# Token layer of a four-layer conv network: the residual in two half tiles, each loaded for the next chunk

## The chip, the cores and the metric

The kernel runs on one core of one Trainium2 chip. The metric is the device time of one launch in microseconds (us). All data is 32-bit float. A core has a matmul engine (PE, with its weight loads PEld), a vector engine (DVE), a scalar engine for activations (ACT), a general engine (POOL) and an engine that here only issues DMAs (SP). Each engine takes its instructions in the order in which the built program lists them, and waits where one of them needs what another engine or a DMA has not yet made.

## The reference

Four layers work on an image of 4 x 48 x 256 x 256. Each normalizes its input over 16 groups of channels and adds its result to that input. The second, the token layer, is the one that changes:

```python
t = x.reshape(B, H * W, dim)                       # 48 consecutive numbers of x are one token
t = gelu(gelu(t @ W1 + b1))                        # 48 -> 16, exact gelu
x1, x2 = t[..., :8], t[..., 8:]
n = layernorm(x2)                                  # over 8 features, then seen as 8 images of 256 x 256
sp = depthwise 3x3 conv(n) + dw_b
ch = 1x1 conv(n) + pw_b
out = (x1 * (sp * ch)) @ W2 + b2                   # 8 -> 48
...
x = x + _L1_conv_ref(_gn(x), ...)                  # the residual: the layer's own input, once more
```

The first layer is a channel attention with 3x3 depthwise convolutions. Layers three and four run recurrences over the rows and the columns of the image.

## The kernel before, in words

The program runs in three stretches. The first computes the attention weights of layer one. The second applies layer one as a convolution in blocks of 16 rows and, from the second image on, runs the token layer of the images that are done beside it. The third is a long recurrence on PE (`ps` L1010) for layers three and four.

In the second stretch a token layer's unit is a chunk of 32 image rows. There are 8 chunks to an image and 32 in all. `tick(c, conv)` returns pieces that are emitted one after the other. Tick c works on three chunks at once. It transposes the tokens of chunk c+1 (`load`, `relay`, `transposed`). It computes the hidden features and the norm of chunk c (`hidden`, `centered`, `normed`). For chunk `old` = c-2 it computes the gate and the output (`shift`, `gate`, `add_b2`, `output`, `finish`). Between them it calls `conv` four times, and each call emits half of a block of layer one, until the blocks run out. So the first 20 ticks that have an output hold two blocks of layer one each, and the last 12 hold the token layer alone.

The order within one engine is not simply the order of emission: the framework reorders instructions by its own estimate of when they can start. All DMAs here go through SP's one queue.

The names that matter:

- `x1` is the layer's input in memory; `load(c)` reads a chunk of it as tokens into `tok` (L726, 1.5 MB in two DMAs, one buffer), `relay` copies it to `pairs` on POOL (L733), `transposed` turns it by PE (`ptok` L739) into `xt` (copies L743 on ACT, L745 on DVE).
- `hidden`: PE `ph` L686, ACT `h` L756, L765, L767. `centered`: PE `pm` L773, DVE `d` L775, POOL `sq` L777. `normed`: PE `pvar` L782, ACT `v` L784, DVE reciprocal L785, DVE `d` L787, ACT `n` L789, then the `near<-n` DMAs L799 to L808.
- `gate`: PE `psp` L818 and L819 (L819 reads `nears`, which POOL fills at L812), PE `pch` L821, ACT `sp` L824, DVE `sp` L825, POOL `g` L827.
- `load_x(c)` reads the chunk's residual into `xr` (L835, two DMAs of 768 KB, one buffer of 96 x 4096). Its partitions hold two image rows of a pair times 48 channels; the free axis holds 16 pairs of rows.
- `add_b2(c)` adds the output bias to the whole tile in place (ACT, L839).
- `output(c, ip)` is called for the even pairs (`ip` 0) and the odd pairs (`ip` 1). It makes four matmuls `pout` into four of the seven PSUM banks (L853) and eight DVE sums `y<-pout,xr` (L864). After `ip` 1 the chunk is written (L872) and `finish` takes its statistics (L883).
- Layer one: `x1n` and `x2n` are the normalized inputs (POOL memsets L527, L528; ACT L529; one buffer each), PE `py` L569 and L578, DVE `y` L592 and statistics L593, DMAs `t<-in_x` L510 to L523 and `x<-y` L598.

Of the kernel before, what the change touches and what calls it, by code (L numbers as in the profile page):

```python
# [9 lines left out]
F32 = mybir.dt.float32  # L10
# [6 lines left out]
B, C, H, W = 4, 48, 256, 256  # L17
G = 16
NP = 2
P = 96  # L20
HW = H * W
R = 16
NB = H // R
RT = 32
KC = 8
# [611 lines left out]
def gated_layer(ctx, tc, banks, p_small, x1, x2, w1, w2, dw, ends, pw, cols, b2, k, coef1, coef2):  # L637
# [6 lines left out]
    nc = tc.nc  # L644
# [3 lines left out]
    res = ctx.enter_context(tc.tile_pool(name="t_res", bufs=1))  # L648
# [4 lines left out]
    items = [(b, j) for b in range(B) for j in range(NJ)]  # L653
# [45 lines left out]
    def strips(b):  # L699

        got = []
        for c in range(2):
            spread = feat.tile([P, G], F32, tag="spread", name="spread")
            nc.vector.tensor_scalar_mul(spread, k["of_group", P], coef1[b][:, c : c + 1])
            ps = p_small.tile([128, G], F32, tag="small", name="pstrip")
            nc.tensor.matmul(ps, lhsT=k["ones", P], rhs=spread, start=True, stop=True)
            t = feat.tile([128, G], F32, tag=f"strip{c}", name=f"strip{c}")
            nc.vector.tensor_copy(t, ps)
            got.append(t)
        scale[b] = got[0]  # L710
        bias[b] = feat.tile([128, 2, G], F32, tag="bias", name="bias")
        for half in range(2):
            nc.vector.tensor_scalar(
                bias[b][:, half, :], got[1], csum[:, half : half + 1], col[:, half : half + 1], ALU.mult, ALU.add
            )

    toks, pairs, xts = {}, {}, {}
    h1s, h2s, ds, sqs, gs, xrs, ys, stats = {}, {}, {}, {}, {}, {}, {}, {}

    def load(c):  # L720
        b, j = items[c]
        t = toks[c] = tok.tile([128, R, 4 * C], F32, tag="tok", name="tok")
        flat = x1[b].rearrange("c n -> (c n)")[j * 2 * R * W * C : (j + 1) * 2 * R * W * C]
        src = flat.rearrange("(k r t n) -> k t r n", k=2, r=R, t=T)
        for kk in range(2):
            nc.sync.dma_start(t[kk * T : (kk + 1) * T], src[kk])  # L726

    def relay(c):

        m = pairs[c] = tok.tile([128, 4, R, C], F32, tag="pairs", name="pairs")  # L730
        t = toks.pop(c).rearrange("p r (q e) -> p q r e", q=4)
        for r in (0, R // 2):
            nc.gpsimd.tensor_copy(m[:, :, r : r + R // 2, :], t[:, :, r : r + R // 2, :])  # L733
# [15 lines left out]
    def hidden(c, half):  # L749
        b, j = items[c]  # L750
        ph = banks.tile([128, CH], F32, tag="bank", name="ph")
        project(ph, half, lambda t: xts[c, t])
        h = feat.tile([128, CH], F32, tag=f"hid{half}", name="h")
        for kk in range(2):
            g = 2 * j + kk
            nc.scalar.activation(  # L756
                by_token(h)[:, kk],
                by_token(ph)[:, kk],
                AF.Gelu,
                bias=bias[b][:, half, g : g + 1],  # L760
                scale=scale[b][:, g : g + 1],
            )
        if half == 0:
            h1 = h1s[c] = feat.tile([128, 2, W], F32, tag="h1", name="h1", bufs=4)
            nc.scalar.activation(h1.rearrange("p k (t q) -> p k q t", q=4), by_token(h), AF.Gelu)  # L765
        else:
            nc.scalar.activation(h, h, AF.Gelu)  # L767
            h2s[c] = h

    def centered(c):  # L770
        pm = banks.tile([128, CH], F32, tag="bank", name="pm")
        h2 = h2s.pop(c)
        nc.tensor.matmul(pm, lhsT=k["mean8", 128], rhs=h2, start=True, stop=True)  # L773
        d = ds[c] = feat.tile([128, CH], F32, tag="d", name="d")
        nc.vector.tensor_sub(d, h2, pm)  # L775
        sq = sqs[c] = feat.tile([128, CH], F32, tag="sq", name="sq", bufs=1)
        nc.gpsimd.tensor_mul(sq, d, d)  # L777
# [32 lines left out]
    def shift(c):  # L810
        for dx in range(3):
            nc.gpsimd.tensor_copy(shifted[c % 2][32 * dx : 32 * dx + 2 * F], near[c % NN][:, :, dx : dx + W])  # L812
# [13 lines left out]
        g = gs[c] = feat.tile([128, 2, W], F32, tag="g", name="g")  # L826
        nc.gpsimd.tensor_mul(flat(g), flat(h1s.pop(c)), sp)  # L827

    def load_x(c):
        b, j = items[c]  # L830
        t = xrs[c] = res.tile([P, 2, R // 2, W], F32, tag="xr", name="xr")
        src = x1[b].rearrange("c (h w) -> c h w", w=W)[:, 2 * j * R : 2 * (j + 1) * R, :]
        src = src.rearrange("c (k i r) w -> r c k i w", k=2, r=2)
        for r in range(2):
            nc.sync.dma_start(t[r * C : (r + 1) * C], src[r])  # L835

    def add_b2(c):
        t = xrs[c]
        nc.scalar.activation(t, t, AF.Identity, bias=b2_sb)  # L839

    def output(c, ip):
        b, j = items[c]
        if ip == 0:

            ys[c] = res.tile([P, NK, 2, R, KC], F32, tag="y1", name="y1")
            if j == 0:
                stats[b] = feat.tile([P, NJ * 8, 6], F32, tag="st", name="st1")
        y, t, g = ys[c], xrs[c], gs[c]
        ps = []
        for q in range(4):  # L850
            p = banks.tile([P, 2, W], F32, tag="bank", name="pout")
            here = slice(32 * q, 32 * q + 32)
            nc.tensor.matmul(  # L853
                p.rearrange("p k (q v) -> p k q v", q=2),
                lhsT=w2_sb[here, ip, :],
                rhs=g[here].rearrange("p k (v q) -> p k q v", q=2),
                start=True,
                stop=True,
            )
            ps.append(p)  # L860
        for q in range(4):
            i = 2 * q + ip
            for kk in range(2):
                nc.vector.tensor_add(  # L864
                    y[:, :, :, kk * R // 2 + i, :].rearrange("p a q w -> p q a w"),
                    ps[q][:, kk].rearrange("p (q a w) -> p q a w", q=2, a=NK),
                    t[:, kk, i, :].rearrange("p (a w q) -> p q a w", w=KC, q=2),
                )
        if ip == 0:
            return  # L870
        gs.pop(c)
        nc.sync.dma_start(  # L872
            x2[b // 2][:, b % 2, :, j * R : (j + 1) * R, :].rearrange("p a h w -> p a (h w)"),
            y.rearrange("p a q h w -> p (a q) (h w)"),
        )
# [3 lines left out]
    def finish(c):  # L879
        b, j = items[c]  # L880
        flat = ys.pop(c).rearrange("p a q h w -> p (a q h w)")
        for i in range(8):
            nc.vector.bn_stats(stats[b][:, j * 8 + i, :], flat[:, i * 512 : (i + 1) * 512])  # L883
        if j == NJ - 1:
            mv = feat.tile([P, 2], F32, tag="mv1", name="mv1")
            nc.vector.bn_aggr(mv, stats.pop(b).rearrange("p a b -> p (a b)"))
            after.extend(k.group_norm_pieces(feat, p_small, mv, "mean6", coef2[b]))

    def tick(c, conv):

        n, old = len(items), c - 2
        now, was, new = 0 <= c < n, 0 <= old < n, c + 1 < n

        def first():
            if c < 0:
                load(c + 1)
            if new:  # L900
                relay(c + 1)
            if was:
                load_x(old)
                shift(old)
            while after:
                after.pop(0)()

        def last():
            if c + 2 < n:
                load(c + 2)  # L910

        pieces = [first]
        if now:
            if items[c][1] == 0:
                pieces.append(lambda: strips(items[c][0]))
            pieces += [lambda: hidden(c, 1), lambda: hidden(c, 0)]
        if was:
            pieces.append(lambda: gate(old))
        pieces.append(conv)
        if now:  # L920
            pieces.append(lambda: centered(c))
        if new:
            pieces += [lambda i=i: transposed(c + 1, i) for i in range(2)]
        if was:
            pieces += [lambda: add_b2(old), lambda: output(old, 0)]
        pieces.append(conv)
        if new:
            pieces += [lambda i=i: transposed(c + 1, i) for i in range(2, 4)]
        if now:
            pieces.append(lambda: normed(c))  # L930
        if was:
            pieces.append(lambda: output(old, 1))
        pieces.append(conv)
        if new:
            pieces += [lambda i=i: transposed(c + 1, i) for i in range(4, NI)]
        if was:
            pieces.append(lambda: finish(old))
        pieces += [conv, last]
        if c == n + 1:
            pieces.append(lambda: [piece() for piece in after])  # L940
        return pieces
# [503 lines left out]
```

## Time and profile before

| what | value |
|---|---|
| median of 4 runs | 9557.14 us (9549.5 to 9560.55) |
| the profiled execution's own time | 9560.55 us |
| its span from first to last instruction | 9558.5 us |
| mean granted clock of PE | 0.957 |
| PE busy | 8768.3 us, 92% of the span |
| DVE, ACT, POOL busy | 4395.0, 3317.3, 1449.0 us |
| first `xr` load to last sum of the token layer | 2107 to 3564 us |
| chunk writes L872 in ticks with layer one | 20, from 2143.3 to 3180.1 us |
| chunk writes L872 in ticks without | 12, to 3564.4 us |

The rows of the profile give an engine, a line of the program, the tile written and the tiles read, a count, and what ended the idle time before. PE's busy time contains modelled ends and so overstates how full it is. The clock that PE was granted is given in parts of full speed.

### The profile page before, as it was taken

To read this page: it belongs to the slowest core of one execution; us is meant where nothing else is said; L and a number is where in the kernel's file an instruction comes from. 1 tells how busy PE (TensorE), PEld (TensorE's weight loads), DVE (VectorE), ACT (ScalarE), POOL (GpSimd) and SP (SyncE) were. 2 spreads that over 40 slices of the span, in tenths; PEclk is the share of its full clock that TensorE was granted. 3 is DMA by queue.
4 is the path that set the end of the run, shared out by engine and by line. 5 is a ranking of instruction groups with operands and counts; after the bars stand their busy time and mean duration, and the time that the engine had idled before them with its cause. 6 is when DMAs were issued, how large, how long until landed. Compare 5 with 4: busy or idle time off the path is not lost.

```text
span 9558.5 us, 160394 instructions
## 1 busy us (share of the span) xinstructions
PE 8768.3 (92%) x62920; PEld 7269.5 (76%) x62920; DVE 4395.0 (46%) x10806; ACT 3317.3 (35%) x7021; POOL 1449.0 (15%) x2850
## 2 busy tenths in 40 slices
PE   6999999989999759999999999999999999976980
PEld 5777777333333229999999999999999999966980
DVE  3331011335554554445556665556655555533550
ACT  0000010223333437546652246632256622243101
POOL 0000000001111110000003320023300033311460
PEclk9999999999999879999999999999999999987995
DMA  7653322668888768656647776557676567588669
GB/s 153 132 127 79 69 67 60 134 140 176 172 173 177 155 133 154 144 126 163 150 123 183 192 158 161 140 146 189 169 163 157 141 151 193 145 194 195 168 175 200
DMA packets 1033974, 1440.81 MB, mean 151 GB/s; under 512 B 63952, under 2 KB 955600, under 8 KB 965632
## 3 DMA queue, kind: packets, MB, share of 16 engines
q1 hardware_dynamic: 1033120, 1430.22, 65.7%
q8 instruction: 493, 8.08, 0.4%
q14 instruction: 265, 2.17, 0.1%
q0 software_dynamic: 96, 0.33, 0.0%
HBM read 837.19 MB, written 534.77 MB: 144 GB/s over the span
## 4 chain that ended last, share of the span: by engine, by line
PE 85%; DMA 7%; DVE 2%; SPq 2%; ACT 2%; issue 1%; POOL 0%; ACTq 0%; DVEq 0%; POOLq 0%
PE ps L1010 57%; PE py L569 5%; PE acc L283 5%; PE acc L284 5%; PE acc L285 3%; PE py L578 3%; DMA col<-U 2%; DMA oi<-x 2%; DMA tok<-x 2%; PE pt L265 1%; DMA xr<-x 1%; PE ptok L739 1%; PE ph L686 1%; PE pout L853 1%; ACT xr L839 1%
## 5 line engine op out<-in xcount | busy, mean ns | idle before, releaser
L1010 PE MATMUL ps<-carry,w 96*96 96x128 f32 x48960 | 5522.0, 275 | 191.0 <-DVE carry L1018 163.9
L1010 PEld LDWEIGHTS ps<-carry,w 96*96 96x96 f32 x48960 | 5432.4, 163 | 279.9 <-DVE carry L1018 187.7
L1018 DVE SCALAR_TENSOR_TENSOR carry<-ps,b,col 96x128 f32<-96x128 f32 x4080 | 1787.6, 440 | 1335.7 <-PE ps L1010 1141.7
L1221 POOL TENSOR_TENSOR stage<-stage,carry 96x128 f32<-96x128 f32 (+1 forms) x2044 | 1060.4, 520 | 4225.7 <-DVE carry L1018 4106.5
L1191 ACT COPY col<-carry 96x128 f32<-96x128 f32 x2040 | 845.3, 425 | 774.4 <-DVE carry L1018 763.6
L1131 ACT COPY up<-carry 96x128 f32<-96x128 f32 x1792 | 528.3, 298 | 1537.5 <-DVE carry L1014 1537.3
L1014 DVE TENSOR_TENSOR carry<-ps,dn 96x128 f32<-96x128 f32 x2280 | 656.2, 288 | 750.1 <-PE ps L1010 631.2
L1090 ACT ACTIVATE dn<-carry,b 96x128 f32<-96x128 f32 (+1 forms) x2044 | 791.9, 399 | 332.5 <-DVE carry L1014 282.6
L569 PE MATMUL py<-x1n,wy 128*96 128x512 f32 x1536 | 717.7, 617 | 33.8 <-ACT x1n L529 29.2
L1014 DVE TENSOR_TENSOR carry<-ps,up 96x128 f32<-96x128 f32 x1792 | 509.2, 287 | 503.9 <-ACT up L1131 376.8
L284 PE MATMUL acc<-xs,xt 128*96 128x288 f32 x2048 | 667.0, 408 | 0.0
L283 PE MATMUL acc<-xt 128*96 128x288 f32 x2048 | 666.3, 409 | 0.0
L569 PEld LDWEIGHTS py<-x1n,wy 128*96 128x96 f32 x1536 | 249.5, 169 | 470.6 <-issue 452.6
L268 DVE COPY xt<-pt 128x384 f32<-128x384 f32 x256 | 136.6, 554 | 851.1 <-PE pt L265 651.2
L285 PE MATMUL acc<-xt,xs 128*96 128x192 f32 x2048 | 501.8, 327 | 0.0
L250 ACT ACTIVATE xn<-raw,coef 96x2048 f32<-96x2048 f32 x64 | 133.6, 2094 | 986.0 <-PE pt L265 819.0
L285 PEld LDWEIGHTS acc<-xt,xs 128*96 128x96 f32 x2048 | 332.3, 165 | 154.5 <-issue 1.8
L284 PEld LDWEIGHTS acc<-xs,xt 128*96 128x96 f32 x2048 | 332.1, 165 | 151.2 <-issue 2.4
L592 DVE TENSOR_TENSOR y<-py,t 96x512 f32<-96x512 f32 x256 | 169.9, 678 | 439.4 <-PE py L578 439.4
L578 PE MATMUL py<-x2n,wy 64*96 64x512 f32 x1536 | 361.9, 601 | 6.7 <-ACT x2n L529 6.7
L283 PEld LDWEIGHTS acc<-xt 128*96 128x96 f32 x2048 | 330.5, 165 | 5.6 <-issue 1.5
L578 PEld LDWEIGHTS py<-x2n,wy 64*96 64x96 f32 x1536 | 117.7, 159 | 239.3 <-issue 238.4
(176 smaller groups left out, 4163.9 us busy)
## 6 DMA issues: line engine op xcount, KB each, us to landing
stage<-x SPq DMA_DIRECT2D x64, 1536.0 KB
x<-stage SPq DMA_DIRECT2D x64, 1536.0 KB
dn<-x SPq DMA_DIRECT2D x240, 384.0 KB
col<-U SPq DMA_DIRECT2D x60, 1536.0 KB
R<-col SPq DMA_DIRECT2D x60, 1536.0 KB
col<-R SPq DMA_DIRECT2D x60, 1536.0 KB
D<-dn SPq DMA_DIRECT2D x56, 1536.0 KB
up<-D SPq DMA_DIRECT2D x56, 1536.0 KB
```

What stands on the lines that cost most here:

```text
L283: nc.tensor.matmul(acc[0], lhsT=xt[:, h + 2, :], rhs=xt[:, here, :], start=first, stop=last)
L284: nc.tensor.matmul(acc[1], lhsT=xt[:, h + 2, :], rhs=xs[:, here, :], start=first, stop=last)
L285: nc.tensor.matmul(acc[2], lhsT=xs[:, h + 2, :], rhs=xt[:, past, :], start=first, stop=last)
L569: nc.tensor.matmul(ps, lhsT=held["w"][0][:, dx], rhs=x1n[:, 2 * c : 2 * c + 2, dx : dx + W], start=dx == 0, stop=False)
L578: nc.tensor.matmul(held["ps"][q + 2 * s], lhsT=held["w"][1][here, dx], rhs=x2n[here, 2 * q : 2 * q + 2, dx : dx + W], start=False, stop=dx ...
L1010: nc.tensor.matmul(ps, lhsT=w_sb[layer][:, way, j, :], rhs=old[:, i, j : j + W // 2], start=j == 0, stop=j == 2)
L1014: nc.vector.tensor_add(new[:, i].rearrange("p (k w) -> p k w", w=KC), ps.rearrange("p (k w) -> p k w", w=KC), inp[:, i])
L1018: nc.vector.scalar_tensor_tensor(new[:, i], ps, b_sb[layer][:, way : way + 1], inp[:, i], ALU.add, ALU.add)
L1090: nc.scalar.activation(inp[:, b], blocks(new[:, b]), AF.Identity, bias=bias[:, 0:1])
L1131: nc.scalar.copy(place[:, b], blocks(new[:, b]))
L1191: nc.scalar.copy(col[:, b], new[:, b])
L1221: nc.gpsimd.tensor_add(to[:, b], to[:, b], new[:, b])
```

## The change

The tile `xr` becomes two half tiles of 96 x 2048, one for the pairs of each parity (`xr0`, `xr1`), with one buffer each. `load_x(c, ip)` fills one of them by two DMAs of 384 KB. It is no longer called at the start of the tick that uses it. `output(c, ip)` calls it for chunk c+1 after it has emitted the eight sums that read the half tile. The first chunk's halves are loaded at the end of tick 1. `add_b2` works on each half by itself. The bytes, the matmuls and the sums are the same.

```diff
-    def load_x(c):
+    def load_x(c, ip):
+        if c >= len(items):
+            return
         b, j = items[c]
-        t = xrs[c] = res.tile([P, 2, R // 2, W], F32, tag="xr", name="xr")
+        t = xrs[c, ip] = res.tile([P, 8, W], F32, tag=f"xr{ip}", name="xr")
         src = x1[b].rearrange("c (h w) -> c h w", w=W)[:, 2 * j * R : 2 * (j + 1) * R, :]
-        src = src.rearrange("c (k i r) w -> r c k i w", k=2, r=2)
+        src = src.rearrange("c (q i r) w -> i r c q w", i=2, r=2)
         for r in range(2):
-            nc.sync.dma_start(t[r * C : (r + 1) * C], src[r])
-    def add_b2(c):
-        t = xrs[c]
+            nc.sync.dma_start(t[r * C : (r + 1) * C], src[ip, r])
+    def add_b2(c, ip):
+        t = xrs[c, ip]
         nc.scalar.activation(t, t, AF.Identity, bias=b2_sb)
...
-        y, t, g = ys[c], xrs[c], gs[c]
+        y, t, g = ys[c], xrs.pop((c, ip)), gs[c]
...
-                    t[:, kk, i, :].rearrange("p (a w q) -> p q a w", w=KC, q=2),
+                    t[:, 4 * kk + q, :].rearrange("p (a w q) -> p q a w", w=KC, q=2),
                 )
+        load_x(c + 1, ip)
         if ip == 0:
             return
...
             if was:
-                load_x(old)
                 shift(old)
...
         def last():
+            if old == -1:
+                for ip in range(2):
+                    load_x(0, ip)
             if c + 2 < n:
                 load(c + 2)
...
-            pieces += [lambda: add_b2(old), lambda: output(old, 0)]
+            pieces += [lambda: [add_b2(old, ip) for ip in range(2)], lambda: output(old, 0)]
```

In the changed program the line numbers of the touched steps are L838 (load), L842 (bias), L856 (`pout`), L867 (sums), L876 (chunk write) and L887 (statistics).

The framework's reordering gives the changed program these orders on the engines. They are read from the built programs.

- PE, ticks with layer one: before, `pm` L773 stood between the first quarter's L569 and L578; now it stands after L578.
- DVE, the same ticks: `d<-h,pm` L775 stood ahead of that quarter's two `y` L592 and two statistics L593; now it stands behind them. The eight sums of `ip` 0 stand behind the next `xt` copy L745, and three of `ip` 1 stand ahead of the reciprocal L785.
- ACT, the same ticks: the block's `x1n` L529 stood ahead of `sp` L824; now it stands behind it. The next block's `x1n` and `x2n` stand ahead of `v` L784. One half's bias stands between `v` and `n` L789, the other between the last `xt` copy and the first `h`; both belong to the next chunk.
- SP, the same ticks: `tok` x2, seven `t` loads, `xr0` x2, `x<-y` x2, one `t` load, `near` x4, `xr1` x2, the chunk write, six `t` loads, `x<-y` x2.
- Ticks without layer one: both biases stand ahead of `v` L784 (before: one, behind `n` L789). On DVE the sums of `ip` 0 stand ahead of the reciprocal in some ticks and behind it in others, those of `ip` 1 behind `d` L787. On PE L819 stands behind `pch`, `pm` and the first `ptok`. On SP `tok` stands behind the chunk write.

## The prediction

> **What bounds it now.** The chain that ended last says which engine to watch: PE has 85% of it, and the residual's load appears at 1%. I then asked the tile `xr` for its instructions and its waiters.
>
> ```profile
> PE 85%; DMA 7%; DVE 2%; SPq 2%; ACT 2%; issue 1%; POOL 0%; ACTq 0%; DVEq 0%; POOLq 0%
> L839 ACT ACTIVATE xr<-xr,b_sb x32: 3662/3708/3711, 2122.8 to 3555.3; 96x4096 f32<-96x4096 f32 x32
>   DMA xr<-x: 92.0, 21
>   DVE y L864: 197.1, 28
>   PE pout L853: 106.3, 12
> ```
>
> The bias waits 92.0 us for its DMA, the sums wait 197.1 us for the bias, `pout` 106.3 us for banks that the sums hold. These overlap; they are no gain to add up. So next the timeline: first a tick with layer one, and one tick (from 2557) that differs.
>
> ```profile
> 2557.59 1.97 PE L739 MATMUL ptok<-cst,pairs 128*128 128x128 f32 x8 [4.15 <-POOL pairs L733]
> 2574.43 6.96 PE L569 MATMUL py<-x1n,wy 128*96 128x512 f32 x12 [2.25 <-ACT x1n L529]
> 2601.38 5.36 PE L569 MATMUL py<-x1n,wy 128*96 128x512 f32 x12 [0.26 <-ACT x1n L529]
> 2607.64 0.69 DVE L775 TENSOR_TENSOR d<-h,pm 128x512 f32<-128x512 f32 x1 [5.04 <-PE pm L773]
> 2611.93 1.09 PE L739 MATMUL ptok<-cst,pairs 128*128 128x128 f32 x8 [1.58 <-POOL pairs L733]
> 2618.02 3.71 ACT L839 ACTIVATE xr<-xr,b_sb 96x4096 f32<-96x4096 f32 x1 [4.38 <-DMA xr<-x]
> 2627.76 5.36 PE L569 MATMUL py<-x1n,wy 128*96 128x512 f32 x12 [0.88 <-ACT x1n L529]
> 2634.11 2.82 PE L578 MATMUL py<-x2n,wy 64*96 64x512 f32 x12 [0.98 <-ACT x2n L529]
> ```
>
> Columns: start, length, engine, line, operation; in brackets the idle time and who ended it. PE is nearly full here: 49 of 52.8 us. Its gaps are ACT's fault (the bias, waiting for its DMA, stands ahead of `x1n`) and `pairs`'. The same twelve matmuls take 5.36 us, or about 7 when PE has idled: 13 of 20 ticks have the long form in the middle. Then a tick without layer one, and the very end:
>
> ```profile
> 3303.53 1.02 PE L782 MATMUL pvar<-sq,cst 128*128 128x512 f32 x2
> 3306.35 3.35 DVE L785 RECIPROCAL v<-v 128x512 f32<-128x512 f32 x1 [2.36 <-ACT v L784]
> 3311.62 3.67 ACT L839 ACTIVATE xr<-xr,b_sb 96x4096 f32<-96x4096 f32 x1
> 3315.32 5.39 DVE L864 TENSOR_TENSOR y<-pout,xr 96x256 f32<-96x256 f32 x16 [4.82 <-ACT xr L839]
> 3316.13 2.01 PE L853 MATMUL pout<-g,w_sb 32*96 32x512 f32 x2 [8.63 <-DVE y L864]
> 3559.00 5.39 DVE L864 TENSOR_TENSOR y<-pout,xr 96x256 f32<-96x256 f32 x16 [14.96 <-ACT xr L839]
> ```
>
> Here the bias is on the path: behind `n`, ahead of all sums; PE stands 8.63 us for a bank before it may start the next chunk. At the end 14.96 us pass for load and bias.
>
> **Ticks with layer one** (20; 19 intervals between chunk writes average 54.57 us). Per ordinary tick (16 of them):
>
> 1. Middle, removed. The bias leaves ACT's way, so `x1n` and `x2n` are ready before PE asks. In the tick shown this is 0.88 + 0.98, and `pout`, held by banks, takes 2.54 instead of 1.15: 3.1 together. In ticks of the long form it is 2.25 + 1.7 = 3.95. I take -3.6.
> 2. First quarter, added. `x1n` now stands behind `sp` L824, which needs L819 (ends 2600.26). 0.69 for `sp` and 2.05 for `x1n` end at 2603.0; PE is free at 2601.1. Idle 1.9 instead of 0.26: +1.6. After 2.25 us of idling the twelve matmuls took the long form each time, after 0.88 sometimes: half of 1.7. +2.5, bounds 1.6 and 3.3.
> 3. First `ptok`, added. `d` stands behind `y`, `y` and two statistics: 2.74, then `d` 0.69, `sq` 1.04, and `pairs`, which POOL takes behind `sq`, 1.46: 5.9 from L578's end to `ptok`, against 1.58. Since `pm` (0.95) moves behind L578 and runs inside that wait: +3.4. At the lower clock `ptok` takes 1.97 for 1.09 and `pout` 1.57 for 1.16: +1.3. Sum +4.7. Low bound 2.7, from the tick at 2557, which has this `pm` order already; high 6.4, if the next L569 is long too.
> 4. DMA, at nothing. `xr0` goes into a hole (the queue is nearly idle from 2623 to 2637). `xr1` goes ahead of the chunk write, so `tok` has 5.63 MB in front of and in it instead of 5.25, less the early `t` load: 27 us become 29 and it lands about 1.8 us before `pairs` wants it. If that cover is gone, up to 1.9 us a tick. SP waits at `xr0` and `xr1` for sums; `x<-y` and the chunk write queue behind and wait for DVE anyway.
> 5. Two biases of 96x2048 for one of 96x4096: 2.05 by the 128x2048 row, so 4.1 for 3.7, in ACT's idle time.
>
> Sum -3.6 + 2.5 + 4.7 = +3.6, times 16 = +58. Four ticks (57.6 on average, around image changes) have item 3 already: -3.6 + 0.7 = -2.9 each, -12. Together +46; bounds -10 and +98.
>
> [...] The rows above show long matmuls after 2.25, and others after 0.87; I follow the rows.
>
> **Ticks without layer one.** Eight intervals, 3223.7 to 3482.2, mean 32.3. Both biases now run on loads made a tick earlier. L819 comes later on PE by `pch`, `pm` and `ptok`, so `g` and `pvar` come 2.8 later (`pvar` ends at 3307.3 instead of 3304.5). Where the even sums stand ahead of the reciprocal (3 ticks), banks are free: `pout` 1.25, `ptok` 1.1, the next `ph` at 3309.7 instead of 3319.97, a tick of 22.5. Where they stand behind it (5 ticks), the last `pout` waits: reciprocal to 3312.5, one sum 0.36, `pout` 0.5, `ptok` 1.97, a tick of 28. 3 x 22.5 + 5 x 28 = 208 against 258.5: -51. What is late next is the DMA queue: 4.5 MB a tick, and 3 MB took 14.8 us from 3320.7, so 22 us. The tick at the change-over (43.6): -5, judged by the same bank wait of 5.7. The last three ticks, 31.1 + 25.2 + 25.9: without the bias the first is bound by reciprocal and sums (24), the second by `near`, `nears` and L819 (15.5), the third by statistics 4.84, `sp` 0.75 and sums 5.4 (11.5): -31. Together -87, bounds -50 and -115 (all eight ticks of one kind or the other).
>
> [...]
>
> **Sum.** 9560.55 + 46 - 87 = 9520. The profiled run lies 3.4 us above the median of the four; I leave that inside the range.
>
> **Rivals.**
> - Both kinds of tick gain: item 3 does not bite because `tok` is what `pairs` waits for anyway (0.97 at 2610.4 speaks for it, 4.15 at 2557 against). Ordinary ticks then end near zero: 9460 to 9480.
> - Slower: the odd half's bias now stands on ACT ahead of the first `h`. `xr1` is issued behind `near`, 24.5 us after `ptok`; a 1.5 MB `tok` on an empty queue took 10.0 us (3346.8 to 3356.8), so half of it some 6; bias 2.05 and table load 1.28 end at 33.8, and `ph` gives `h` its input at 34.1. Slack 0.3. If the load meets a queue still full of `t` and `x<-y`, each us beyond that delays `h`, `sp` and `x1n`, hence PE, in 20 ticks: 4 us make 9520 + 74, about 9595. It decides from 3.3 us (9580). For it: in the busy stretches `xr` landed 15.55 us after its issue; against it: the queue is idle from 2632 to 2635.
> - The wait is not removed but moved: `pout` still finds no bank without layer one. Then only the last ticks gain, 31 + 5: about 9570.
>
> **Numbers.** Forecast 0.48 (own range 9490 to 9550, from item 3's bounds; 0.34 of it faster, 0.14 same), both gain 0.20, slower 0.22, moved 0.10 (0.04 same, 0.06 slower: at 9570 the bounds of the ticks with layer one decide). 0.2% is 19 us, about what a measurement can tell. Faster 0.54, same 0.18, slower 0.28. The range 9455 to 9595 takes in the first rival, and the second as far as 4 us.
>
> **What would show it.** Right: sums no longer wait for `xr`; about 7.06-us L569s vanish from the middle of ticks and appear in the first quarter; `ptok` idles 4 to 6 us for `pairs` in every tick with layer one; chunk writes lie 57 to 59 us apart there, 22 to 28 without. Wrong: a bias on ACT that still waits for its DMA, or `h` late behind it (I count 0.3 us of slack), or tail ticks above 30 us.

## The result and the profile after

| | before | after |
|---|---|---|
| median | 9554.57 us (53 runs) | 9564.64 us (33 runs) |
| span of the profiled execution | 9558.5 us | 9565.2 us |
| mean of the 19 intervals between chunk writes with layer one | 54.57 us | 56.84 us |
| interval at the change-over | 43.6 us | 33.0 us |
| the eight intervals that follow | 258.5 us | 246.3 us |
| from there to the end of the last sums | 82.2 us | 63.9 us |

The ratio is 1.001, with a 95% interval from 1.0005 to 1.0015: the change costs about 10 us, where 9520, 35 below this median of before, was forecast. In the two traces the stretch of the token layer grows by 6 us: the first chunk write is 4.0 later, the 19 intervals bring +43.2, the change-over -10.6, the eight intervals -12.3, the last ticks -18.3.

First the same parts of the page and the answer on the tile `xr` as were read of before, now of the kernel after (its bias is L842, its `pout` L856, its sums L867):

```profile
PE 57%; DMA 4%; SPq 1%; ACT 0%; issue 0%; DVE 0%; POOL 0%; ACTq 0%; DVEq 0%; POOLq 0%
L842 ACT ACTIVATE xr<-xr,b_sb x64: 1951/1992/2007, 2107.6 to 3560.5; 96x2048 f32<-96x2048 f32 x64
  DMA xr<-x: 105.1, 22
  PE pout L856: 22.9, 7
```

The chain could be followed back only part of the way here (its shares sum to some 63%), so its 57% is not set against the 85% of before. The tile's answer says more. The 197.1 us that the sums waited for the bias are gone, and `pout` waits 22.9 us for banks instead of 106.3. The bias still waits for its DMA, 105.1 us, but that is ACT waiting alone (e6 below shows by how little). So the change does what it says, and the time has to be looked for elsewhere. The timeline of a tick with layer one:

```profile
2660.47 2.00 ACT L842 ACTIVATE xr<-xr,b_sb 96x2048 f32<-96x2048 f32 x1 [5.50 <-DMA xr<-x]
2664.19 1.02 ACT L756 ACTIVATE h<-ph,bias,strip 128x256 f32<-128x256 f32 x2 [0.43 <-PE ph L686]
2672.30 7.06 PE L569 MATMUL py<-x1n,wy 128*96 128x512 f32 x12 [1.99 <-ACT x1n L529]
2682.03 1.13 PE L773 MATMUL pm<-h,cst 128*128 128x512 f32 x2
2684.53 0.67 DVE L775 TENSOR_TENSOR d<-h,pm 128x512 f32<-128x512 f32 x1
2687.78 1.97 PE L739 MATMUL ptok<-cst,pairs 128*128 128x128 f32 x8 [4.62 <-POOL pairs L733]
```

The middle of the tick has lost its gaps. In their place stand 1.99 us ahead of the first L569 and 4.62 us ahead of the first `ptok`, and the matmuls behind them take the long form (7.06, 1.97). Now a tick without layer one:

```profile
3340.62 2.36 PE L686 MATMUL ph<-xt,w_sb 128*32 128x512 f32 x12
3352.47 1.04 POOL L777 TENSOR_TENSOR sq<-d 128x512 f32<-128x512 f32 x1 [8.79 <-DVE gn_m L89]
3353.46 1.89 POOL L812 COPY nears<-near 16x512 f32<-16x512 f32 x3
3355.41 2.08 PE L819 MATMUL psp<-nears,ends_sb 80*128 80x512 f32 x2 [0.31 <-POOL nears L812]
3360.45 2.13 PE L856 MATMUL pout<-g,w_sb 32*96 32x512 f32 x8 [2.97 <-POOL g L827]
3366.65 3.35 DVE L785 RECIPROCAL v<-v 128x512 f32<-128x512 f32 x1 [2.29 <-ACT v L784]
3370.66 2.02 PE L856 MATMUL pout<-g,w_sb 32*96 32x512 f32 x2 [2.85 <-DVE y L867]
3374.51 2.06 PE L686 MATMUL ph<-xt,w_sb 128*32 128x512 f32 x9
3389.35 2.08 PE L819 MATMUL psp<-nears,ends_sb 80*128 80x512 f32 x2 [2.86 <-POOL nears L812]
```

(Here and below, the last row of a timeline can end with the stretch of time that was read, and then shows fewer instructions than the group has: nine `ph` here.)

From `ph` to `ph` this tick takes 33.9 us, not 28. No bias is waited for. What is late is L819, 14.8 us behind `ph`, because `nears` on POOL comes behind `sq`; from there `g`, `pout`, `pvar`, the reciprocal and the last `pout` follow each other, with short idles of PE between them and matmuls of 2 us for 1. In this tick PE also waits 2.14 us for group statistics (L96) just ahead of L819; in the tick behind it, whose L819 is the last row, it waits 2.86 us for `nears` alone. Four of the eight ticks are of this kind, with L819 14.8 to 15.7 us behind `ph`; in the kernel before it comes 9.0 to 10.2 us behind.

### The profile page after: what moved, and what is told of

Its sections match the earlier page's. It is cut to its first block, busy times and chain, and to the rows that moved or that the text cites. A ratio compares the mean times of both kernels' runs of the same rounds, so it can differ in the third digit from the quotient of the medians.

```text
span 9565.2 us, 160531 instructions
## 1 busy us (share of the span) xinstructions
PE 8772.4 (92%) x62920; PEld 7271.3 (76%) x62920; DVE 4398.9 (46%) x10806; ACT 3335.1 (35%) x7053; POOL 1449.9 (15%) x2850
## 4 chain that ended last, share of the span: by engine, by line
PE 57%; DMA 4%; SPq 1%; ACT 0%; issue 0%; DVE 0%; POOL 0%; ACTq 0%; DVEq 0%; POOLq 0%
PE ps L1016 57%; DMA col<-U 2%; DMA oi<-x 2%; SPq L1291 1%; ACT oo L1308 0%; SPq L1167 0%; DMA dn<-x 0%; DMA x<-y 0%; DVE y L867 0%; SPq L1044 0%; DVE carry L1024 0%; DMA U<-carry 0%; DMA x<-stage 0%; DVE carry L1020 0%; SPq L1174 0%
## 5 line engine op out<-in xcount | busy, mean ns | idle before, releaser
L569 PE MATMUL py<-x1n,wy 128*96 128x512 f32 x1536 | 719.3, 619 | 31.6 <-ACT x1n L529 29.9
L569 PEld LDWEIGHTS py<-x1n,wy 128*96 128x96 f32 x1536 | 250.9, 170 | 476.2 <-issue 462.5
L592 DVE TENSOR_TENSOR y<-py,t 96x512 f32<-96x512 f32 x256 | 171.4, 677 | 602.4 <-PE py L578 596.9
L578 PE MATMUL py<-x2n,wy 64*96 64x512 f32 x1536 | 361.9, 601 | 0.0
L578 PEld LDWEIGHTS py<-x2n,wy 64*96 64x96 f32 x1536 | 116.7, 158 | 234.1 <-issue 233.9
```

Source lines behind the costliest of these rows:

```text
L569: nc.tensor.matmul(ps, lhsT=held["w"][0][:, dx], rhs=x1n[:, 2 * c : 2 * c + 2, dx : dx + W], start=dx == 0, stop=False)
L578: nc.tensor.matmul(held["ps"][q + 2 * s], lhsT=held["w"][1][here, dx], rhs=x2n[here, 2 * q : 2 * q + 2, dx : dx + W], start=False, stop=dx ...
```

## The experiments

The theory, ORDER: the early load removes the wait for the residual; what that wins is paid back by the order in which the framework then lists the instructions (`pm` and `d` late, `x1n` behind `sp`, `nears` and L819 late). The rival TRANSFERS: loads of half the size, put ahead of other loads, cost it. The rival BIASES: two biases on ACT hold up `n` or `h`. Times below are medians, set against the runs of the kernel before that shared their chip (9554.1, 9555.6 and 9557.4 in the three sets). Line numbers shift by up to 22 in kernels with added lines, and the diffs are shortened. Where an order is forced, it is an edge without a semaphore, which only tells the framework what to list first:

```diff
+def queued(tc, inst, behind):      # list inst after SEEN[behind] on its engine
+    if behind in SEEN:
+        tc.add_manual_dep(inst.ins, SEEN[behind].ins.name, ...NoSync..., reason="order")
+    return inst
```

| run | what is different | median, us | ratio to before, 95% interval | mean tick with layer one | eight ticks without |
|---|---|---|---|---|---|
| e1 | after, `x1n` ahead of `sp` | 9466.03 | 0.9908 (0.9892 to 0.9923) | 51.39 | 243.3 |
| e2 | after, `pm` and `d` first | 9470.94 | 0.9911 (0.9896 to 0.9926) | 51.35 | 244.1 |
| e3 | after, `nears` and L819 first | 9543.21 | 0.9989 (0.998 to 0.9998) | 56.80 | 217.6 |
| e4 | all three | 9428.0 | 0.987 (0.9857 to 0.9884) | 51.08 | 226.6 |
| e5 | split, loads as before | 9517.97 | 0.996 (0.9947 to 0.9972) | 54.18 | 249.5 |
| e6 | early load, no split | 9647.85 | 1.0095 (1.0081 to 1.0109) | 61.81 | 230.3 |
| e7 | before, `pm` and `d` late | 9629.41 | 1.0076 (1.0063 to 1.0089) | 58.19 | 259.0 |
| e8 | e4, `tok` in mid-tick | 9434.19 | 0.987 (0.9855 to 0.9885) | 52.46 | 219.7 |
| e9 | early load only without layer one | 9512.83 | 0.9954 (0.994 to 0.9968) | 53.74 | 248.1 |
| e10 | e4, bias behind `sp` in the tail | 9410.65 | 0.9846 (0.9833 to 0.986) | 51.17 | 202.6 |
| e11 | e4, `tok` ten us earlier | 9566.55 | 1.0009 (0.9999 to 1.0018) | 58.18 | 227.6 |
| e12 | e10 and e11 together | 9542.47 | 0.9985 (0.9976 to 0.9993) | 58.15 | 210.7 |

### e1: `x1n` first

```diff
-        nc.scalar.activation(v[:, :, 1 : W + 1], t, ...)                 # x1n, x2n
+        SEEN[v.shape[1]] = nc.scalar.activation(v[:, :, 1 : W + 1], t, ...)
-        nc.scalar.activation(sp, flat(psp), ...)
+        queued(tc, nc.scalar.activation(sp, flat(psp), ...), 8)          # behind x1n
```

> The kernel after, with one edge of order on ACT: sp (L824) is queued behind the x1n that stands before it in the program, so x1n is made first as in the kernel before. In the built program PE then also takes pm between L569 and L578, and DVE takes d ahead of the layer-one sums, again as before. Theory ORDER (the early load does remove the wait, and what it wins is paid back by the order that the framework then chooses): ticks with layer one fall from 58.3 to about 51 us, 16 times 7.2 = 115 us, so about 105 us below the kernel before, near 9450. The 1.99 us ahead of the first-quarter L569 and the 4.62 us ahead of the first ptok fall to 0.3 and 1.6. Rival TRANSFERS (half-tile loads ahead of the chunk write and tok delay tok, and pairs waits for tok): ptok still idles 3 us or more, with pairs released by tok's DMA; at most 2.5 us a tick from x1n, 40 us, so 30 below the kernel before at best. Rival BIASES (two biases on ACT that wait for their DMA hold n and h): within 20 us of the kernel before.

Measured: 9466.03, 88 below before, 99 below after. The ticks with layer one take 51.39 us on average for 56.84. One edge on ACT was enough to bring `pm` and `d` back to the front as well, as the listing of the built program showed beforehand. TRANSFERS and BIASES fall as causes of the loss: the loads and the biases are untouched. The expected 105 were not all there, and POOL shows why. Of this kernel:

```profile
2640.60 2.87 POOL L747 COPY pairs<-tok 128x1536 f32<-128x1536 f32 x2 [1.59 <-DMA tok<-x]
```

Now `sq` is early, and `tok` is what `pairs` waits for: 23.6 us in 17 ticks over the 19 intervals, where the kernel after had 1.7 us in one. TRANSFERS is the next bound behind ORDER.

### e2: `pm` and `d` first

```diff
-        pieces.append(conv)
-        if now:
-            pieces.append(lambda: centered(c))
+        pieces.append(lambda: conv((lambda: centered(c)) if now else None))
     ... in conv, ahead of the third piece (the L578s and their sums):
+                between()                                      # centered(c)
+                with tc.issue_after(SEEN["pm"].ins), tc.issue_after(SEEN["d"].ins):
+                    made[u][3 * q + 2]()
```

> The kernel after with only pm and d moved: pm is emitted between the L569 and the L578 matmuls of the first conv piece, and edges of order queue the L578s behind pm and the layer-one sums behind d. sp still stands ahead of x1n. ORDER: item 3 of the prediction alone is undone, 4.7 us in 16 ticks, 75 us: about 65 below the kernel before, near 9490; the first ptok idles 1.6 us for pairs, and the 1.99 us ahead of the first-quarter L569 stays. TRANSFERS: ptok goes on idling 3 us or more, now for tok, and the time stays within 20 us of the kernel before. BIASES: as TRANSFERS for the time, but the idle time of PE shows n or h as what came last.

Measured: 9470.94, 83 below before, more than the 65 expected. The 1.99 us ahead of the first L569 stay, and 7.06-us L569s with them, yet the mean tick is that of e1. So `sp` ahead of `x1n` costs next to nothing once `pm` is first: while PE is held there (25.9 us over the 19 intervals, 10.8 in e1), `tok` comes in, and `ptok` then waits 14.0 us in all for `pairs` instead of 38.0 in e1.

### e3: `nears` and L819 first

```diff
+            SEEN["nears"] = nc.gpsimd.tensor_copy(shifted[c % 2][...], near[c % NN][...])
-        nc.gpsimd.tensor_mul(sq, d, d)
+        queued(tc, nc.gpsimd.tensor_mul(sq, d, d), "nears")
+        SEEN["psp"] = nc.tensor.matmul(psp, lhsT=ends_sb, ...)           # L819
-        nc.tensor.matmul(pch, lhsT=pw_sb, ...)
+        queued(tc, nc.tensor.matmul(pch, lhsT=pw_sb, ...), "psp")
```

> The kernel after with two edges of order that act in the ticks without layer one: on POOL sq is queued behind the nears that stands before it in the program, on PE pch behind L819, so that L819 comes before pch and pm again. The ticks with layer one keep after's order and length (58 us). ORDER: L819 comes 10 us after ph instead of 14.8, the eight intervals without layer one fall from a mean of 30.8 to between 24 and 28, 24 to 56 us, so 15 to 45 below the kernel before. TRANSFERS (22 us of queue in a tick) would not show below 22 and says nothing against this. BIASES (in these ticks the bias of the even half stands ahead of the second h or of sp on ACT): the intervals stay at 30 or more, and PE waits for ACT.

Measured: 9543.21, 11 below before. The eight intervals fall from 246.3 to 217.6 (27.2 each on average, within the expected 24 to 28), the stretch from there to the end of the last sums from 63.9 to 56.3; the ticks with layer one stay at 56.80. That is 35 us out of the trace of the stretch; the median moved by 21 against after and lies just outside the expected 15 to 45 below before. The trace of e3 reached the second stretch some 7 us later (its first L569 starts at 1639.3, that of after at 1632.2), and its first chunk write comes 12 us later; why is open.

### e4: all three orders

The edits of e1, e2 and e3 together.

> The three edits of the other runs of this set together: after's loads in the order of before. ORDER: 115 and 24 to 56 us below the kernel after, so 130 to 160 below the kernel before, 9395 to 9425. TRANSFERS: no more than the tail part, 15 to 75 below the kernel before. BIASES: within 30 us of the kernel before.

Measured: 9428.0, 126 below before, 137 below after, 3 us above the expected stretch. All of after's loads and biases are in it. Order alone decides whether they gain 1.3% or lose 0.1%. The time, the busy time of PE, its clock, the share of the DMA engines and the GB/s, over the 19 intervals with layer one, of after and of this run:

```profile
2147.30:3227.20 1079.90, 966.80 (x3484) 0.93 0.75 167
```

```profile
2153.90:3124.60 970.70, 917.32 (x3484) 0.99 0.84 186
```

The same 3484 matmuls take 49 us less of PE's busy time, at a granted clock of 0.99 for 0.93 (before: 0.96), and some 60 us of idle time are gone too.

### e5: the split alone

```diff
+            if was:
+                for ip in range(2):
+                    load_x(old, ip)              # in first(), as the kernel before
-        load_x(c + 1, ip)                        # in output()
```

> The split alone: two half tiles as in the kernel after, both loaded where the kernel before loads the whole tile (start of the tick that uses them). In the built program pm and d stand as in the kernel before; in the ticks without layer one both biases stand between v and n. ORDER: the gain and the loss both hang on the early load, so the ticks with layer one stay at 53 to 56 us and the sums go on waiting for the bias; in the tail 4 us of bias ahead of n make the ticks longer, 33 to 36. 0 to 45 us above the kernel before. TRANSFERS (half-tile loads are what cost the kernel after its gain): ticks with layer one at 57 us or more here too, 45 or more above the kernel before.

Measured: 9517.97, 38 below before, where 0 to 45 above were expected. The ticks with layer one gain little (54.18 for 54.57, within the expectation). The gain is in the ticks without, where a loss was expected: 249.5 for 258.5 in the eight, 58.9 for 82.2 at the end. In the eight ticks this is again order. ACT and DVE of one of them:

```profile
3291.30 3.88 ACT L842 ACTIVATE xr<-xr,b_sb 96x2048 f32<-96x2048 f32 x2
3294.70 2.67 DVE L867 TENSOR_TENSOR y<-pout,xr 96x256 f32<-96x256 f32 x8
```

Both biases now stand ahead of `n` and run while DVE makes the reciprocal (to 3294.78), so the even sums follow it at once; before, the bias stood behind `n` and the sums waited 4.82 us for it. The loads are issued behind the chunk write, as before. In the last ticks the half tile itself helps: it is free as soon as its own eight sums are made (one load is issued at 3484.49, ahead of the odd sums), and the first sums wait for one half alone, at most 3.90 us where they waited 14.22 and 14.96. Half-size loads cost nothing that shows; TRANSFERS falls a second time.

### e6: the early load alone

```diff
+        load_x(c + 1)                            # in output(c, 1), behind the odd sums
-                load_x(old)                      # in first(); the first chunk's in last()
```

> The early load alone: one whole tile and one bias as in the kernel before, loaded for the next chunk when the odd sums are made. The built program has after's order in the ticks with layer one (pm behind the L578s, sp ahead of x1n) and before's order in the others, but with the bias ahead of n. ORDER: ticks with layer one at 57 to 59 us as in the kernel after, although nothing is split; without layer one the bias no longer waits for its load, 28 to 31 us. Between the kernel before and 40 us above it. TRANSFERS: without half-size loads the ticks with layer one fall below 54, and the kernel lies 20 or more below the kernel before.

Measured: 9647.85, 92 above before; at most 40 were expected. Without layer one the early load does what was expected of it (230.3 for 258.5). With layer one the ticks take 61.81, 5 more than the late order explains. ACT and PE of one such tick:

```profile
2584.14 3.71 ACT L841 ACTIVATE xr<-xr,b_sb 96x4096 f32<-96x4096 f32 x1 [10.69 <-DMA xr<-x]
2595.34 1.14 PE L569 MATMUL py<-x1n,wy 128*96 128x512 f32 x1 [4.69 <-ACT x1n L529]
```

The whole tile lands 10.69 us after ACT is ready for it, its bias stands ahead of the first `h`, and `h`, `sp` and `x1n` move back with it. This is the slower rival of the prediction, at the price of a tile twice as large. The kernel after escapes it by a hair: its odd half's bias waits too, 5.50 us in the tick shown, but `h` then still waits 0.43 us for PE, and 0.06 to 1.60 us in the 19 ticks from 2154 us on.

### e7: the late order in the kernel before

```diff
-        nc.tensor.matmul(pm, ...)
+        queued(tc, nc.tensor.matmul(pm, ...), "py")      # behind the last L578 of the piece
-        nc.vector.tensor_sub(d, h2, pm)
+        queued(tc, nc.vector.tensor_sub(d, h2, pm), "st")  # behind its last statistic
```

> The kernel before with one part of after's order forced on it and nothing else: pm queued behind the L578 matmuls of the first conv piece, d behind the layer-one sums and statistics. Loads, biases and the rest stand as in the kernel before. ORDER by item 3 of the prediction: 4.7 us in 16 ticks, 75 us above the kernel before, at least 2.7, 43 us. If instead the late pm costs only together with the early loads: within 15 us of the kernel before.

Measured: 9629.41, 74 above before (9555.62 in this set), with 75 expected. Over the 19 intervals `ptok` waits 85.7 us for `pairs` (36.2 before), and PE also 42.4 us for `x1n` (28.0 before), so not all of the 74 is the gap ahead of `ptok`. Neither load nor bias was touched, and the same gap stands in the same place:

```profile
2634.06 1.12 PE L787 MATMUL pm<-h,cst 128*128 128x512 f32 x2
2636.56 0.67 DVE L789 TENSOR_TENSOR d<-h,pm 128x512 f32<-128x512 f32 x1
2639.80 1.54 PE L753 MATMUL ptok<-cst,pairs 128*128 128x128 f32 x6 [4.62 <-POOL pairs L747]
```

### e8: `tok` loaded in mid-tick

```diff
+        if c + 2 < n:
+            pieces.append(lambda: load(c + 2))   # ahead of output(old, 0)
-            if c + 2 < n:
-                load(c + 2)                      # in last()
```

> The kernel with all three orders restored, and tok for the chunk after next loaded in the middle of the tick, ahead of the even half's load, instead of at its end. In that kernel the first ptok still idles 36 us in all for pairs in the ticks with layer one, and pairs waits 61 us for tok: TRANSFERS is the next bound there, by this reading. Then pairs is made before it is wanted, ptok does not idle at the start, and 25 to 45 us go: 9385 to 9405, 150 to 170 below the kernel before. If the queue is full instead, xr or t come late behind tok, x1n or the sums wait for them, and the time stays within 15 us of 9428.

Measured: 9434.19, level with e4. In the ticks with layer one, `ptok` no longer waits for `pairs` (36.0 us in e4), but PE waits 38.1 us for `x1n`, which waits 35.9 us for `t` (6.9 in e4) and 24.0 for `tok`. (Of the 61 us that the expectation names for `pairs` in e4, 28.0 lie in the 19 intervals.) The wait changed its name. The second branch of the expectation holds: at 181 GB/s on average (186 in e4), the load that goes earlier makes another go later.

### e9: early only without layer one

```diff
+    early = lambda c: c >= 21
+        if early(c + 1):               # in output()
+            load_x(c + 1, ip)
+                if not early(old):     # in first(): both halves, as in e5
```

> The halves of the kernel after, but only the chunks of the ticks without layer one (chunk 21 on) are loaded early; the others are loaded at the start of the tick that uses them, as in the run of the split alone. ORDER, if the two stretches add: the ticks with layer one as in the split alone (mean 54.2), the eight intervals behind them as in the kernel after (246) with its last ticks, 10 to 15 us shorter in all than the split alone: about 9505, 50 below the kernel before. If the stretches do not add (the loss of the ticks with layer one comes from elsewhere): 9550 or more.

Measured: 9512.83, 45 below before, 50 expected. The two stretches do add: the ticks with layer one are near those of e5 (53.74 for 54.18), the eight intervals near those of after (248.1 for 246.3). But the early load brings nothing here on top of the split alone. From the change-over on, the trace of e9 is 5.7 us longer than that of e5; after's late `nears` has come with it (PE waits 11.8 us for it, 2.2 in e5). That the median lies 5 us below e5 comes from the ticks with layer one, where nothing was meant to differ, and the two 95% intervals overlap.

### e10: both biases behind `sp`

```diff
+        SEEN["sp"] = queued(tc, nc.scalar.activation(sp, ...), 8)
-        nc.scalar.activation(t, t, AF.Identity, bias=b2_sb)
+        queued(tc, nc.scalar.activation(t, t, ...), "sp" if c > 19 else None)
```

> The kernel with all three orders restored, and in the ticks without layer one both biases queued behind sp on ACT. There the even half's bias (2.0 us) stands between the first and the second hidden half, ahead of the last h and of sp, and pout waits 29.3 us (10 times) for g, which needs sp. BIASES, as a second-order cost: sp comes 1 to 2 us earlier in 8 to 10 ticks, 8 to 20 us, 9408 to 9420. If g waits for L819 or POOL instead: within 8 us of 9428.

Measured: 9410.65, 17 below e4 and 147 below before (0.9846), as expected: the best version here. A tick of e3, which has the bias of e4's tail, and one of this run:

```profile
3393.43 1.99 ACT L856 ACTIVATE xr<-xr,b_sb 96x2048 f32<-96x2048 f32 x1
3396.21 0.64 ACT L838 ACTIVATE sp<-psp,col 128x512 f32<-128x512 f32 x1
3399.10 2.13 PE L870 MATMUL pout<-g,w_sb 32*96 32x512 f32 x8 [3.50 <-POOL g L841]
```

```profile
3317.76 0.64 ACT L846 ACTIVATE sp<-psp,col 128x512 f32<-128x512 f32 x1
3318.31 3.88 ACT L864 ACTIVATE xr<-xr,b_sb 96x2048 f32<-96x2048 f32 x2
3320.66 1.25 PE L878 MATMUL pout<-g,w_sb 32*96 32x512 f32 x8 [1.84 <-POOL g L849]
```

With the bias out of `sp`'s way `pout` idles 1.84 instead of 3.50, and runs in 1.25 us for 2.13. So BIASES was a real cost, but a small one; with layer one e10 and e4 are alike (51.17 and 51.08). The eight intervals come down to 202.6.

### e11 and e12: `tok` ten us earlier

```diff
+            SEEN["tok"] = nc.sync.dma_start(t[kk * T : (kk + 1) * T], src[kk])
+            queued(tc, nc.sync.dma_start(t[r * C : (r + 1) * C], src[ip, r]), "tok")   # xr
+            pieces.append(lambda: load(c + 2))   # ahead of output(old, 1)
-                load(c + 2)                      # in last()
```

> The kernel with all three orders restored, and tok's two halves issued about ten us earlier, one ahead of the near DMAs and one ahead of the odd half of xr and of the chunk write. ptok's first wait for pairs (36 us in the ticks with layer one) goes. If only the order of the queue delays tok: 15 to 30 us less, 9398 to 9413. If the queue is full in these ticks (186 GB/s on average), t and x1n are late in its place, as when tok went ahead of the even half: 9423 to 9443.

> The two edits of the runs on the bias and on tok together, as a candidate that beats both kernels. If both work, 23 to 50 us below 9428; if only the bias works, 9408 to 9420; if neither, 9420 to 9440.

Measured: 9566.55 and 9542.47. The first lies 139 above e4. Both lie outside everything expected; only the direction is that of the full queue. ACT and PE in one tick of e11:

```profile
2674.53 2.00 ACT L864 ACTIVATE xr<-xr,b_sb 96x2048 f32<-96x2048 f32 x1 [11.36 <-DMA xr<-x]
2687.06 5.25 PE L569 MATMUL py<-x1n,wy 128*96 128x512 f32 x6 [8.55 <-ACT x1n L529]
```

The odd half of `xr` was pushed behind `tok`; its bias ends 6.2 us after `ph` has started, against 0.3 in the kernel after, and holds `h`, `sp` and, with a late `t`, `x1n`: `x1n` itself waits 60.7 us for `t` over the 19 intervals (6.9 in e4), so the late bias is one cause of two. The ticks with layer one go from 51.08 to 58.18. This is the slower rival once more, in a kernel that has the halves: `tok` ahead of the odd half was enough. e12 keeps the bias' gain in the tail (210.7 for 227.6) and the loss of e11 in the rest.

## Why the prediction was wrong, point by point

- **What bounds the kernel.** Right: the wait of the sums for the bias went, and PE's gaps in mid-tick with it.
- **The sums.** In item 1 the three terms of the tick shown add up to 3.25, not 3.1. Two bounds do not come out of their terms: items 2 and 3 at theirs give about 0 and +86 for the ticks with layer one, where -10 and +98 stand, and eight ticks of 28 us give -70 for the rest, where -50 stands. None of this decides the outcome.
- **Ticks with layer one, the sum.** Forecast +46, measured +47 (4.0 and 43.2). The order was read correctly from the built program, and e7 puts item 3, in the kernel before, at 74 us where 16 x 4.7 = 75 were reckoned.
- **Item 1.** e4, which has the early loads in the old order, takes 3.49 us per tick less than before; the terms -3.6 and -2.9 average to -3.5 over 16 and 4 ticks.
- **Item 2, mis-sized.** Forecast +2.5 a tick. The 1.99 us are there (1.9 forecast), but e2 and e4, which differ by them, are 0.27 us a tick apart. Its idle time is covered by what `ptok` would otherwise wait for `tok`. Item 3 is larger in turn: e2, which undoes it alone, takes 5.5 us a tick out of after. The right sum had two wrong sizes in it, which cancelled: that was luck.
- **Item 4.** Zero was right: where `pm` is late, `pairs` waits 1.7 us in all for `tok` over the 19 intervals. The cover was named with its price should it go, and went in e1, as soon as `sq` was early.
- **Ticks without layer one: the step that failed.** "`g` and `pvar` come 2.8 later", and with it ticks of 22.5 and 28 us. The order on PE alone was counted (`pch`, `pm`, `ptok` ahead of L819: 2.8). That POOL makes `nears` behind `sq` was not: in four of the eight ticks L819 came 14.8 to 15.7 us behind `ph` instead of 9.0 to 10.2. In the tick shown `pvar` ends 25.3 us behind `ph`, in the prediction's tick of before 17.4, so 7.9 later and not 2.8: late L819, 2.97 us of idling for `g`, and matmuls in the long form. The eight intervals lost 12 us instead of 51, and five of them are longer than the 30 us that the prediction named as a sign of being wrong. e3 undoes this order and comes to 217.6 (e4, with the same two edges, to 226.6; that difference is open). The even bias, which stands ahead of `sp` on ACT, cost nothing in the tick shown, where `sp` waits 1.61 us for L819; with L819 early it was the next bound, and e10 moves it too: 202.6, with single ticks of 22.4 and 23.1. The prediction reckoned 208, but with L819 2.8 late, so the nearness is partly chance.
- **The last ticks.** Forecast -31, measured -18: late `nears` again (e3 gives 7.6 back), and the last sums wait 4.55 us for the chunk write that still reads `y`, which the sum left out. The change-over gave -10.6 for -5.
- **The rivals.** "Both kinds gain" fell: `tok` is not what `pairs` waits for in the kernel after. "Moved (no bank)" has the nearest time, 9570, but not the mechanism: `pout`'s wait for banks fell to 22.9. "Slower" needs the odd bias 3.3 us later than in the kernel after, whose slack of 0.43 in the tick shown was reckoned as 0.3; e6 and e11 brought it about, and their ticks are 5 and 7 us longer (in e11 `t` is late as well).
- **Where the expected gain went.** It is there (126 us of it in e4, 147 in e10; 38 come with the split alone, e5), and in the kernel after it is spent again on order that the edit does not name: 5.5 us a tick with layer one on `pm` and `d`, 29 us in the eight ticks without on `nears`. `x1n` behind `sp` costs next to nothing by itself (e2), but the edge that undoes it brings `pm` back too (e1).

The long form does not follow from the length of the idle time alone: in the kernel after, one and the same idle of 1.99 to 2.02 us is followed by twelve L569s of 5.36 us five times and of about 7 us ten times. (The long ones after 0.87 us that the prediction speaks of are three of nine in the trace of before; its rows do not show them.) The columns of e4 again, for the kernel after, around the L569 at 2672.30 (7.06 us) and the one at 2389.99 (5.36 us):

```profile
2669.14:2672.55 3.41, 1.42 (x4) 1.00 1.09 328
2672.55:2675.96 3.41, 3.41 (x5) 0.50 1.11 211
2385.83:2389.24 3.41, 2.17 (x6) 1.00 1.13 259
2389.24:2392.65 3.41, 2.66 (x7) 1.00 1.10 286
```

In this trace the granted clock is 1.00 or 0.50 and changes only on a grid of 3.41 us, which these stretches follow: from the first chunk write to the last, each of its times at 0.50 lasts 3.41 us or a whole multiple of it. The first idle of 1.99 us lies in one stretch, and the next one has half the clock; the second is parted into 1.24 and 0.75, and the clock stays. Between the first and the last chunk write, 45 stretches at full clock were followed by half: PE had idled 1.69 us or more in 44 of them, 1.07 in one. In the 292 followed by full it had idled at most 1.75. So in this trace the two part at 1.69 to 1.75 us of idling, about half a stretch, and the same 2 us were followed by the long form or not by where they fell. In the trace of before this is less sharp: 12 of 35 fell after less than 1.69 us, down to 0.40; why is open.

The prediction's sum has no term for the size of the loads, 384 KB for 768 KB. In the trace of before the DMA engines moved 199 GB/s from 2617 to 2620 us, where `t` loads of 384 KB and less stand behind `xr`, and 193 GB/s in the six us ahead of that, with `xr`. The halves loaded at the old place gained 38 us (e5), and the whole tile loaded early is 83 us slower than the halves loaded early (e6 against after). This does not measure the size alone, since halves also come free earlier; a whole tile loaded early with the old order restored was not run.

## What to carry to other kernels

When a load is moved forward under a framework that orders instructions by its own estimates, compare the order of every engine, POOL and ACT included, and price each move where it stands: here the moves cost 137 us together, more than the 126 that the early halves win without them. An edge of order without a semaphore is a cheap way to try it, and one edge can bring others back with it. Before a load is pulled ahead, ask which one it pushes behind: in e8, at 181 GB/s on average (186 in e4), an earlier `tok` left `x1n` waiting 35.9 us for `t` instead of 6.9. A waiting instruction on an engine that serves others made that expensive in e11: ACT idles 11.36 us ahead of the bias in the tick shown, `h` stands behind it, and the ticks, with `t` late as well, take 58.18 us for 51.08.

## What the runs showed of the hardware

- Twelve L569 matmuls take 5.36 us or more after one and the same idle time: in the run of the split alone, from 2188 to 3165 us, idles of 2.50 to 2.52 us are followed by 5.36 five times and by 6.80 to 8.37 twelve times. Over the 19 intervals with layer one the granted clock was 0.93 after, 0.96 before and 0.99 in e4, for the same matmuls.
- The early tiles still came later than ACT was ready for them: in e6 two loads of 768 KB, issued from 2573.14 us on, had landed when the bias started at 2584.14, with ACT idle for 10.69 us; in the kernel after two of 384 KB, issued from 2654.66 us on, when it started at 2660.47, with ACT idle for 5.50 us and the DMA engines moving 199 GB/s in between (11.36 us of idling in e11, with `tok` ahead).
